# A four-layer graph network on one core: two more left products in seven blocks, block sums on another engine, and a different priority among ready work

## The chip, the cores and the metric

The kernel runs on one core of a Trainium2 chip. A core has five engines that work side by side, each on its own queue of instructions: TensorE (in the profile PE, with its weight loads as PEld), VectorE (DVE), ScalarE (ACT), GpSimd (POOL) and SyncE (SP), which here only issues DMAs. The metric is the device time of one execution in microseconds (us), the median of three runs.

## The reference

Input `x` is 64 graphs of 256 nodes with 128 features, in fp32, and `adj` a symmetric 256 x 256 matrix of zeros and ones. Four layers follow each other, each of the form `x = layernorm(x + layer(x, adj))`. The two that the change touches are:

```python
# layer 2: a gated unit, five steps; in_matrix = out_matrix = adj
m_in = jnp.einsum('nm,bmd->bnd', in_matrix, h)
m_out = jnp.einsum('nm,bmd->bnd', out_matrix, h)
av = jnp.concatenate([m_in, m_out], axis=-1)
u3 = h @ u3_w.T + u3_b
z = jax.nn.sigmoid(av @ w3_w.T + w3_b + u3)
r = jax.nn.sigmoid(av @ w4_w.T + w4_b + u3)
hv = jnp.tanh(av @ w5_w.T + w5_b + (r * h @ u5_w.T + u5_b))
h = (1.0 - z) * h + z * hv
# layer 3: powers one to three of adj, for two adjacencies that are both adj
nxt = jnp.einsum('ij,bjc->bic', adj, carry)        # three times
y_1 = jnp.einsum('bnik,iok->bno', x_all, weight_1) # x_all: x and the six products
```

Layers 0 and 1 are attention layers over the same adjacency. All arithmetic is fp32.

## The kernel before

**Tiling.** Two graphs make one unit: `UB = 2`, so there are `NU = 32` units. A unit's state is a 128 x 512 tile, features in the partitions and 2 x 256 nodes in the columns, or node-major, with the four blocks of 128 nodes (two graphs, two halves each) side by side. Ten units are in work at once, each in a lane with its own buffers (`LANES = 10`); matmul results lie in eight PSUM banks that all lanes share.

**The order.** Nothing is issued in the order in which the code is written. `add` (L85) records a task with its engine, an estimated duration, the cells that it reads and writes and, for a cell in PSUM, that it takes a bank (`takes`) or uses one (`banks`). `Plan.run` (L115) then plays the tasks through: at each moment every free engine takes, among its tasks whose inputs are due and for which a bank is free, the one with the smallest key. The key is `first` (L1017): the unit's number times `PERIOD` plus the task's due time within the unit; units of the last ten use a denser numbering. `tc.manual_schedule()` issues the result, so the order on each engine is fixed before the run and an instruction whose input is late holds up everything behind it on its engine. The plan's estimate for the time between the end of an instruction and its being seen by another engine (`LATENCY`) is 400 or 500 ns for the compute engines and 4000 for a DMA.

**A left product.** `left` (L812) multiplies a unit by the adjacency directly: for each graph two products of 256 columns, four in a unit. `left_fast` (L820) computes the same from seven products of 128 columns: the 2 x 2 block product with four block sums of the state (`four`, in the buffer `s`; VectorE, L826, L828 and L829), block sums of the matrix prepared once by `fast_blocks` (L466; `adjf` for plain node order and `adjTf` for permuted node order), one copy of the first product by ScalarE to `p1` (L845), and four merging sums by VectorE into `m` (L860, L863, L865, L866). The seven products are those at L833 and use two banks, `x` and `y`. `FAST` (L22) says where this form is used: steps 1 to 4 of layer 2 and (5) the first left product of layer 3. Step 0 of layer 2 uses `left` (L816) with one bank and a ScalarE copy at L886.

`far(u, step)` tells whether a unit's state goes from feature-major to node-major by DMA (through HBM) rather than by TensorE transposes. Units 0 and 1 go by DMA from step 2 on and unit 31 only up to step 0; `left_fast` is used only where `far` holds for the step before.

**A step of layer 2** (L868 to L958): the left product `m`; four 512-column products for the gates (`product`, L890, weights `gT`), the first of which, `gT[3]` with the old state, needs no `m` and follows the second matmul of the left product in the recorded dependencies; one more with `u5T`; three tanh on ScalarE (L901, L909, L918) and four `scalar_tensor_tensor` on VectorE (L904, L916, L920, L922), each over 128 x 512.

**Layer 3** (L970): the left product `aT`; then eight 256-column products with `w3` (L991), which holds the matrix for the part that needs no further adjacency and, beside it, the one for the part that is multiplied by the squared adjacency; ScalarE copies the second part to `s` (L995); four 256-column products with the squared adjacency `a2T` (L998) accumulate onto the first part in PSUM; `layernorm` reads the sum from PSUM. Units 30 and 31 use `layernorm_last`.

`layernorm` (L575): statistics on VectorE (L582), then for most units three small operations and a power on GpSimd (L584, L587, L593, L595), then ScalarE writes the normalised `x` (L606).

Of the kernel before, what the change touches and what calls it, by code (L numbers as in the profile page):

```python
# [13 lines left out]
P = 128  # L14
NEG = -1.0e30
EPS = 1e-5
STEPS = 5
# [1 line left out]
LEAD = 10  # L19
BANKS = 8  # L20
BL = 32
FAST = (1, 2, 3, 4, 5)  # L22
NORM = (0, 1, 2, 3)
SCALES = True
SMALL = ("ve", "cu", "d", "elu", "shift")
# [12 lines left out]
DIRECT_ROWS = 3  # L38
XDIRECT = 10
START = 35e3  # L40
R2 = 1
R3 = 1.5

# [157 lines left out]
def kernel(  # L201
# [42 lines left out]
    def sb(name, shape):  # L244
        return const.tile(shape, F32, tag=name, name=name)

    def cell(name, shape):
        return Cell(sb(name, shape))
# [4 lines left out]
    def bank():  # L253
        return Cell(bank=True)

    def mm_ns(cols, n=1):
        return n * (cols * 1.667 + 5)
# [115 lines left out]
            add(DVE, 200 + 100 * n, lambda: nc.vector.tensor_scalar_mul(t.ap, views(), scale), (ps,), (t,))  # L373
        return t

    adjT = cell("adjT", [P, NC, N])
    ps_adj = bank()
    for mc in range(NC):
        for ic in range(NC):
# [73 lines left out]
    add(POOL, 300, lambda: nc.gpsimd.tensor_scalar_mul(bias2.ap[:, 0:2], bias2.ap[:, 0:2], 0.5), (bias2,), (bias2,))  # L453


    adjTp, adj_p = cell("adjTp", [P, NC, N]), cell("adj_p", [P, NC * NC, BL, P // BL])
    add(ACT, 600, lambda: nc.scalar.copy(
        adj_p.ap, adj_t.ap.rearrange("p i (m q j) -> p (i m) j q", m=NC, j=BL)), (adj_t,), (adj_p,))
    ps_adjp = bank()
# [3 lines left out]
                ps_adjp.ap[:, mc * N + ic * P : mc * N + (ic + 1) * P],  # L463
                adj_p.ap[:, ic * NC + mc].rearrange("p j q -> p (j q)"), ident.ap), (adj_p, ident), (ps_adjp,))
    add(ACT, 500, lambda: nc.scalar.copy(adjTp.ap.rearrange("p c n -> p (c n)"), ps_adjp.ap), (ps_adjp,), (adjTp,))
    def fast_blocks(name, mat):  # L466


        f = cell(name, [P, 2 * NC, N])

        def block(k):
            return f.ap.rearrange("p k (c n) -> p (k c) n", c=NC)[:, k]

        add(ACT, 500, lambda: nc.scalar.copy(f.ap[:, 0:NC], mat.ap), (mat,), (f,))
        for out, (i, op, j) in {4: (1, ALU.subtract, 0), 6: (3, ALU.add, 1), 5: (6, ALU.subtract, 0)}.items():
            add(POOL, 480, lambda out=out, i=i, op=op, j=j: nc.gpsimd.tensor_tensor(block(out), block(i), block(j), op=op),
                (f,), (f,))

        add(POOL, 350, lambda: nc.gpsimd.tensor_scalar_mul(block(5), block(5), -1.0), (f,), (f,))
        add(POOL, 480, lambda: nc.gpsimd.tensor_add(block(7), block(5), block(2)), (f,), (f,))  # L480
        return f

    adjTf = fast_blocks("adjTf", adjTp)
    adjf = fast_blocks("adjf", adjT) if 0 in FAST or STEPS in FAST else None


    plan.rank = R3
    w3 = cell("w3", [D, 2, 2, D])
    add(POOL, 480, lambda: nc.gpsimd.tensor_add(w3.ap[:, 0, 0, :], wk.ap[:, :, 0], ident.ap), (wk, ident), (w3,))
    for k in range(1, 4):  # L490
        add(POOL, 480, lambda k=k: nc.gpsimd.tensor_add(
            w3.ap[:, k % 2, k // 2, :], wk.ap[:, :, k], wk.ap[:, :, k + 3]), (wk,), (w3,))

    a2T = cell("a2T", [P, NC, N])
    ps_a2 = bank()
    for mc in range(NC):
        for kc in range(NC):
# [2 lines left out]
                start=(kc == 0), stop=(kc == NC - 1)), (adj_t, adjT), (ps_a2,))  # L500
    add(DVE, 600, lambda: nc.vector.tensor_copy(a2T.ap.rearrange("p c n -> p (c n)"), ps_a2.ap), (ps_a2,), (a2T,))

    plan.rank = None


# [2 lines left out]
    def gd(ap):  # L508
        return ap.rearrange("p (g d) -> p g d", g=G)
# [307 lines left out]
                ps.ap[:, b * N : (b + 1) * N], lhs(b, mc), mat.ap[:, mc, :],  # L817
                start=(mc == 0), stop=(mc == NC - 1)), (src, mat), (ps,))

    def left_fast(src, blk, mat, s, p1, m):  # L820


        four = gd(s.ap)
        ss = object()

        add(DVE, 360, lambda: nc.vector.tensor_sub(  # L826
            four[:, 0:2], blk(slice(2, 3)).to_broadcast([P, 2, D]), blk(slice(0, 4, 3))), (src,), (s,), group=ss)
        add(DVE, 220, lambda: nc.vector.tensor_sub(four[:, 2:3], four[:, 1:2], blk(slice(0, 1))), (src, s), (s,), group=ss)  # L828
        add(DVE, 220, lambda: nc.vector.tensor_add(four[:, 3:4], four[:, 2:3], blk(slice(1, 2))), (src, s), (s,), group=ss)  # L829
        x, y = bank(), bank()  # L830

        def one(ps, at, lhs, k, c, cells, after=()):
            add(PE, mm_ns(P) + 4, lambda: nc.tensor.matmul(  # L833
                ps.ap[:, at * P : (at + 1) * P], lhs(), mat.ap[:, k, c * P : (c + 1) * P], start=True, stop=True,
                skip_group_check=True), (*cells, mat), (ps,), after, group=four)

        def a(g):
            return lambda: blk(slice(g, g + 1))[:, 0]

        def sm(k):  # L840
            return lambda: four[:, k]


        one(x, 0, a(0), 0, 0, (src,))
        add(ACT, 280, lambda: nc.scalar.copy(p1.ap[:, 0:P], x.ap[:, 0:P]), (x,), (p1,))  # L845
        one(x, 1, a(1), 1, 0, (src,))
        one(y, 3, a(3), 3, 1, (src,), s.writers[-1:])
        one(y, 1, sm(0), 3, 0, (s,))
        one(y, 0, sm(1), 2, 0, (s,))
        one(x, 2, sm(2), 2, 1, (s,))  # L850
        one(y, 2, sm(3), 1, 1, (s,))
        mv = gd(m.ap)

        ms = object()

        def pv(ps):
            return gd(ps.ap)


        add(DVE, 400, lambda: nc.vector.tensor_tensor(  # L860
            mv[:, 0:4:3], pv(x)[:, 1:3], p1.ap[:, 0:P].rearrange("p (o n) -> p o n", o=1).to_broadcast([P, 2, P]), op=ALU.add),
            (x, p1), (m,))
        add(DVE, 400, lambda: nc.vector.tensor_tensor(  # L863
            mv[:, 1:3], pv(y)[:, 0:2], mv[:, 3:4].to_broadcast([P, 2, P]), op=ALU.add), (y, m), (m,))
        add(DVE, 240, lambda: nc.vector.tensor_add(mv[:, 3:4], pv(y)[:, 0:1], mv[:, 2:3]), (y, m), (m,))  # L865
        add(DVE, 400, lambda: nc.vector.tensor_add(mv[:, 1:3], pv(y)[:, 2:4], mv[:, 1:3]), (y, m), (m,))  # L866

    def layer2(u, L):  # L868
        h, ht = turned(u, L, -1), X[u]
        for step in range(STEPS):  # L870
# [1 line left out]
            fast = step in FAST and far(u, step - 1)  # L872
            ps_m = None if fast else bank()
            if fast and not step:
                left_fast(ht, lambda g: ht.ap.rearrange("p b c d -> p (b c) d")[:, g], adjf, L["r"], L["z"], m)
            elif fast:
                left_fast(ht, lambda g: gd(ht.ap)[:, g], adjTf, L["r"], L["z"], m)
            for b in range(0 if fast else UB):
                if ht is X[u]:
                    left(ps_m, ht, b)  # L880
# [8 lines left out]
            def product(ps, w, c, rhs, start, stop, after=()):  # L889
                add(PE, mm_ns(T), lambda: nc.tensor.matmul(ps.ap, w(), rhs.ap, start=start, stop=stop,  # L890
                                                           skip_group_check=True), (c, rhs), (ps,), after)


            lefts = [t for t in plan.tasks[at:] if t.eng == PE]
            product(ps_g, lambda: gT.ap[:, 3], gT, h, True, False, lefts[1:2])
            product(ps_g, lambda: gT.ap[:, 1], gT, m, False, True)
            r, z, v = L["r"], L["z"], L["v"]

# [71 lines left out]
    def layer3(u, L):  # L970
        xT = turned(u, L, STEPS)
        aT, s = L["m"], L["z"]
        if STEPS in FAST and far(u, STEPS):
            left_fast(X[u], lambda g: X[u].ap.rearrange("p b c d -> p (b c) d")[:, g], adjf, L["r"], L["z"], aT)
            tail = [t for t in plan.tasks[-4:-3]]
        else:
            ps_a = bank()
            for b in range(UB):
                left(ps_a, X[u], b)
            add(ACT, 500, lambda: nc.scalar.copy(aT.ap, ps_a.ap), (ps_a,), (aT,))  # L980
            tail = list(ps_a.writers)

        ps = [bank() for _ in range(NC)]

        def view(c):
            return ps[c].ap.rearrange("p (k b d) -> p k b d", k=2, b=UB)

        for k, src in enumerate((xT, aT)):
            for c in range(NC):
                for b in range(UB):  # L990
                    add(PE, mm_ns(N), lambda k=k, src=src, c=c, b=b: nc.tensor.matmul(  # L991
                        view(c)[:, :, b, :], bn(src.ap)[:, b, c * P : (c + 1) * P], w3.ap[:, k],
                        start=(k == 0 and b == 0), stop=(k == 1), skip_group_check=True), (src, w3), (ps[c],), tail)
        for c in range(NC):
            add(ACT, 300, lambda c=c: nc.scalar.copy(s.ap[:, c * N : (c + 1) * N], ps[c].ap[:, N : 2 * N]), (ps[c],), (s,), group=ps)  # L995
        for c in range(NC):
            for mc in range(NC):
                add(PE, mm_ns(N), lambda c=c, mc=mc: nc.tensor.matmul(  # L998
                    ps[c].ap[:, 0:N], a2T.ap[:, mc, c * P : (c + 1) * P], s.ap[:, mc * N : (mc + 1) * N],
                    start=False, stop=(mc == NC - 1), skip_group_check=True), (a2T, s), (ps[c],))  # L1000
        pairs = [(ps[c], lambda c=c: view(c)[:, 0]) for c in range(NC)]
        if u >= NU - 2:
            layernorm_last(u, pairs)
            return
        layernorm(u, L, pairs, swap=True)
        add("sp", 450, lambda: nc.sync.dma_start(out_u[u], X[u].ap), (X[u],), ())
# [10 lines left out]
    def first(t):  # L1017
        if t.rank is not None:
            return t.rank * PERIOD
        if t.unit < 0:  # L1020
            return t.due - 1e6
        return (t.unit if t.unit < NU - LANES else NU - 1 - LATE - (NU - 1 - t.unit) * TAIL) * PERIOD + t.due

    with tc.manual_schedule():
        for t in plan.run(spawn, range(NU), first):
# [31 lines left out]
```

The softmax here doesn't subtract the row's maximum and nothing guards it: scores larger than these inputs give would overflow.

## Time and profile before

| What | Value |
|---|---|
| Median of three runs (lowest, highest) | 1395.11 us (1395.05, 1396.01) |
| Span of the profiled execution | 1394.1 us |
| ScalarE, the three tanh of layer 2 (L901, L909, L918), 160 each | 687 to 689 ns each |
| VectorE, `scalar_tensor_tensor` of a step (L904 to L922) | 683 to 687 ns each |
| VectorE, block sums: 128x256 (L826), 128x128 (L828, L829) | 411 and 399; 281 to 284 ns |
| VectorE, merging sums L860, L863, L866; L865 | 417, 418, 413; 281 ns |
| GpSimd, 128x128 block sums of the matrices (L476) | 467 and 491 ns |
| GpSimd, the layernorm power (L587), 126 times | 1127 ns |
| ScalarE copies L845, L886, L995 | 267, 585, 370 ns |

The span runs from the first to the last instruction of the profiled execution; the run's time has about one us around it. In the rows of the profile a name like `ps<-adjTf,e` says what is written and what is read, buffer numbers left out; since several names share one buffer, a row can show `e` where the code says `r` or `z`, and `p` where it says `v`. A matmul in fp32 appears as two records, a transpose as one. The mean duration in a group's row runs from a matmul's start to its modelled end, so that following matmuls overlap; their rate shows in how far apart they start. "Idle before" is time that the engine stood idle just before an instruction, with what ended it.

### The profile page before, as it was taken

What the parts mean: (1) busy time and instruction counts of PE and PEld (TensorE: products, weight loads), DVE (VectorE), ACT (ScalarE), POOL (GpSimd) and SP (SyncE); (2) the same over time, 40 slices, a digit from 0 to 9 for tenths busy, and PEclk for the clock granted to TensorE, in tenths of its full rate; (3) what the DMA queues carried; (4) which work ended last, traced back from release to release, by engine and by line L of the source; (5) the groups of instructions that cost most, each with busy time, mean ns of one, the idle gap of its engine ahead of it and who ended that gap; (6) DMA issues with size and microseconds to landing.
All of it is one profiled execution on the core that took longest, in us unless ns stands there. A gap on an engine that the chain in (4) does not pass through costs nothing.

```text
span 1394.1 us, 21842 instructions
## 1 busy us (share of the span) xinstructions
PE 1385.5 (99%) x6537; PEld 963.8 (69%) x6537; DVE 1191.1 (85%) x2849; ACT 911.2 (65%) x2094; POOL 257.9 (18%) x488
## 2 busy tenths in 40 slices
PE   9999999999999999999999999999999999999998
PEld 8776576776666766676676667676666666667776
DVE  6788898999988888888898899889888888999763
ACT  6887636556765767666676778787755555565454
POOL 3111020112112112122121122132111110112212
PEclk9999999999999999999999999999999999999999
DMA  4134554455455454554455555554463543544521
GB/s 126 32 62 99 114 120 86 117 108 131 109 114 112 98 130 95 122 127 102 108 108 111 128 110 110 118 114 103 108 129 94 119 105 86 115 114 106 129 52 47
DMA packets 530068, 147.03 MB, mean 105 GB/s; under 512 B 456480, under 2 KB 495136, under 8 KB 529952
## 3 DMA queue, kind: packets, MB, share of 16 engines
q1 hardware_dynamic: 529152, 145.13, 46.6%
q8 instruction: 52, 0.85, 0.3%
q14 instruction: 64, 0.52, 0.2%
q10 hardware_dynamic: 800, 0.52, 0.1%
HBM read 81.10 MB, written 64.46 MB: 104 GB/s over the span
## 4 chain that ended last, share of the span: by engine, by line
PE 98%; ACT 1%; DVE 1%; DMA 0%; issue 0%; SPq 0%; POOL 0%; POOLq 0%; DVEq 0%; ACTq 0%
PE ps L890 49%; PE ps L833 17%; PE ps L991 8%; PE ps L816 5%; PE ps L738 4%; PE ps L998 4%; PE ps L775 4%; PE ps L787 2%; PE ps L733 2%; PE ps L662 2%; ACT p L711 0%; DMA u<-rowu 0%; PE ps L348 0%; PE ps L955 0%; PE ps L528 0%; PE ps L571 0%
## 5 line engine op out<-in xcount | busy, mean ns | idle before, releaser
L890 PE MATMUL ps<-m,gT 128*128 128x512 f32 x960 | 464.1, 593 | 0.0
L890 PEld LDWEIGHTS ps<-m,gT 128*128 128x128 f32 x960 | 170.8, 190 | 124.9 <-issue 107.8
L909 ACT ACTIVATE e<-ps,bias 128x512 f32<-128x512 f32 x160 | 109.7, 687 | 159.0 <-PE ps L890 156.5
L901 ACT ACTIVATE e<-ps,bias 128x512 f32<-128x512 f32 x160 | 109.9, 687 | 98.9 <-PE ps L890 97.0
L833 PEld LDWEIGHTS ps<-adjTf,ht 128*128 128x128 f32 x726 | 117.6, 191 | 74.3 <-issue 60.1
L584 POOL TENSOR_SCALAR ve<-st 128x4 f32<-128x4 f32 x110 | 36.3, 330 | 690.5 <-DVE st L582 662.3
L890 PE MATMUL ps<-e,u5T 128*128 128x512 f32 x320 | 162.4, 592 | 0.0
L587 POOL TENSOR_TENSOR rstd<-ve,nhalf 128x4 f32<-128x4 f32 x126 | 142.0, 1127 | 66.5 <-DVE ve L584 59.5
L833 PEld LDWEIGHTS ps<-adjTf,e 128*128 128x128 f32 x968 | 127.4, 192 | 19.2 <-issue 17.7
L833 PE MATMUL ps<-adjTf,e 128*128 128x128 f32 x968 | 139.6, 275 | 0.0
L918 ACT ACTIVATE p<-ps,bias 128x512 f32<-128x512 f32 x160 | 110.2, 689 | 40.5 <-PE ps L890 38.4
L833 PE MATMUL ps<-adjTf,ht 128*128 128x128 f32 x726 | 123.7, 275 | 0.3 <-DVE m L860 0.3
L920 DVE SCALAR_TENSOR_TENSOR p<-e,p 128x512 f32<-128x512 f32 x160 | 109.4, 685 | 16.5 <-ACT p L918 16.0
L890 PEld LDWEIGHTS ps<-e,u5T 128*128 128x128 f32 x320 | 59.3, 190 | 61.4 <-issue 51.6
L890 PE MATMUL ps<-xT,gT 128*128 128x512 f32 x192 | 97.5, 594 | 0.4 <-ACT xT L530 0.4
L860 DVE TENSOR_TENSOR m<-ps,e 128x256 f32<-128x256 f32 x152 | 63.0, 417 | 25.1 <-PE ps L833 21.2
L764 ACT ACTIVATE e<-m,esd 128x256 f32<-128x256 f32 x116 | 82.2, 766 | 0.0
L904 DVE SCALAR_TENSOR_TENSOR e<-e,xT 128x512 f32<-128x512 f32 x96 | 65.7, 684 | 15.5 <-ACT e L901 13.5
L863 DVE TENSOR_TENSOR m<-ps,m 128x256 f32<-128x256 f32 x152 | 63.3, 418 | 16.0 <-PE ps L833 14.1
L541 DVE STREAM_TRANSPOSE p<-x 128x512 f32<-128x512 f32 x61 | 67.3, 1104 | 11.1 <-ACT x L606 11.0
L738 PEld LDWEIGHTS ps<-ht,p 128*128 128x128 f32 x512 | 65.9, 190 | 12.9 <-issue 12.0
L738 PE MATMUL ps<-ht,p 128*128 128x130 f32 x512 | 68.5, 274 | 0.0
(191 smaller groups left out, 2784.0 us busy)
## 6 DMA issues: line engine op xcount, KB each, us to landing
hb<-p SPq DMA_DIRECT2D x182, 256.0 KB, 2.3
ht<-hb SPq DMA_DIRECT2D x484, 64.0 KB, 2.6
xT<-hb SPq DMA_DIRECT2D x244, 64.0 KB, 2.5
m<-row SPq DMA_DIRECT2D x58, 256.0 KB, 3.8
hb<-p SPq DMA_DIRECT2D x124, 64.0 KB, 1.8
ht<-hb SPq DMA_DIRECT2D x31, 256.0 KB, 3.0
out_dram<-x SPq DMA_DIRECT2D x30, 256.0 KB, 2.4
m<-in_x_dram SPq DMA_DIRECT2D x88, 64.0 KB, 2.3
```

The lines of the kernel that those rows point to most:

```text
L541: add(DVE, 1050, lambda: nc.vector.transpose(v.ap.rearrange("p (a g i) -> p g a i", g=G, i=BL), X[u].ap.rearrange("p b c (j a) -> p (b c) ...
L587: add(POOL, 1050, lambda: nc.gpsimd.tensor_tensor(rstd.ap, ve.ap, nhalf.ap, op=ALU.pow), (ve, nhalf), (rstd,))
L738: add(PE, mm_ns(D + 2), lambda b=b, ic=ic, kc=kc, yv=yv: nc.tensor.matmul(yv()[:, ic, :], p.ap[:, b * NC + kc, ic * P : (ic + 1) * P], h.a ...
L764: add(ACT, 600, lambda g=g, b=b: nc.scalar.activation(e.ap[:, g, :].rearrange("p (c n) -> p c n", c=NC), ev()[:, b], AF.Prelu, bias=esd.ap ...
L816: add(PE, mm_ns(N), lambda b=b, mc=mc: nc.tensor.matmul(ps.ap[:, b * N : (b + 1) * N], lhs(b, mc), mat.ap[:, mc, :], start=(mc == 0), stop ...
L833: add(PE, mm_ns(P) + 4, lambda: nc.tensor.matmul(ps.ap[:, at * P : (at + 1) * P], lhs(), mat.ap[:, k, c * P : (c + 1) * P], start=True, st ...
L890: add(PE, mm_ns(T), lambda: nc.tensor.matmul(ps.ap, w(), rhs.ap, start=start, stop=stop, skip_group_check=True), (c, rhs), (ps,), after)
L901: add(ACT, 600, lambda ps_g=ps_g, up=up: nc.scalar.activation(r.ap, ps_g.ap, AF.Tanh, bias=bias2.ap[:, 1:2], scale=0.5 / up), (ps_g, bias2 ...
L909: add(ACT, 600, lambda ps_g=ps_g, up=up: nc.scalar.activation(z.ap, ps_g.ap, AF.Tanh, bias=bias2.ap[:, 0:1], scale=0.5 / up), (ps_g, bias2 ...
L918: add(ACT, 600, lambda ps_v=ps_v, up=up: nc.scalar.activation(v.ap, ps_v.ap, AF.Tanh, bias=bias2.ap[:, 2:3], scale=1 / up), (ps_v, bias2), ...
L920: add(DVE, 600, lambda: nc.vector.scalar_tensor_tensor(v.ap, z.ap, 1.0, v.ap, op0=ALU.add, op1=ALU.mult), (v, z), (v,))
L991: add(PE, mm_ns(N), lambda k=k, src=src, c=c, b=b: nc.tensor.matmul(view(c)[:, :, b, :], bn(src.ap)[:, b, c * P : (c + 1) * P], w3.ap[:, k ...
```

## The change

It has four parts. First, step 0 of layer 2 joins `FAST`, so that it uses `left_fast` with `adjf`. Second, a new branch of layer 3 for all but the last three units (`PLAIN = 3`) computes the product with the squared adjacency from seven 128-column products as well; its weights are block sums `a2f`, it adds block sums of `s` on VectorE (`-1` is not in `BY_POOL`), merges into the buffer `ht` in SBUF, and `layernorm` then reads from there. The last three units keep the old form in `layer3_end`, with the two halves of `w3` in the other order. Third, the block sums of the state are GpSimd's in all places named by `BY_POOL`. Fourth, the key of a task on TensorE, ScalarE or VectorE that uses an open bank without taking a new one becomes smaller by 10 us (`HASTE`). Two smaller parts: the block sums of a matrix now share one buffer with the matrix, so that two copies go; and the product with `gT[3]` depends, in the fast form, on the third merging sum in place of the second left matmul.

```diff
-FAST = (1, 2, 3, 4, 5)
+FAST = (0, 1, 2, 3, 4, 5)
+BY_POOL = (0, 1, 2, 3, 4, 5)
+HASTE = {"pe": 10e3, "act": 10e3, "dve": 10e3}
+PLAIN = 3
...
+    def blocks(name):
+        whole = Cell(sb(name, [P, 2 * NC, N]))
+        return whole, Cell(whole.ap[:, 0:NC])
+    adjf, adjT = blocks("adjT")
...
-        add(ACT, 500, lambda: nc.scalar.copy(f.ap[:, 0:NC], mat.ap), (mat,), (f,))
...
-    adjTf = fast_blocks("adjTf", adjTp)
-    adjf = fast_blocks("adjf", adjT) if 0 in FAST or STEPS in FAST else None
+    fast_blocks(adjTf, adjTp)
+    fast_blocks(adjf, adjT)
...
+    fast_blocks(a2f, a2T)
...
+    def block_sums(src, blk, s, by_pool):
+        four = gd(s.ap)
+        ss = object()
+        by, eng = (POOL, nc.gpsimd) if by_pool else (DVE, nc.vector)
+        wide, narrow = (830, 480) if by_pool else (360, 220)
-        add(DVE, 360, lambda: nc.vector.tensor_sub(
+        add(by, wide, lambda: eng.tensor_sub(
             four[:, 0:2], blk(slice(2, 3)).to_broadcast([P, 2, D]), blk(slice(0, 4, 3))), (src,), (s,), group=ss)
-        add(DVE, 220, lambda: nc.vector.tensor_sub(four[:, 2:3], four[:, 1:2], blk(slice(0, 1))), (src, s), (s,), group=ss)
-        add(DVE, 220, lambda: nc.vector.tensor_add(four[:, 3:4], four[:, 2:3], blk(slice(1, 2))), (src, s), (s,), group=ss)
+        add(by, narrow, lambda: eng.tensor_sub(four[:, 2:3], four[:, 1:2], blk(slice(0, 1))), (src, s), (s,), group=ss)
+        add(by, narrow, lambda: eng.tensor_add(four[:, 3:4], four[:, 2:3], blk(slice(1, 2))), (src, s), (s,), group=ss)
...
-            product(ps_g, lambda: gT.ap[:, 3], gT, h, True, False, lefts[1:2])
+            merge = plan.tasks[at:][-4:]
+            product(ps_g, lambda: gT.ap[:, 3], gT, h, True, False, merge[2:3] if fast else lefts[1:2])
...
+        if u >= NU - PLAIN:
+            layer3_end(u, L, xT, aT, s, tail)
+            return
+        x, y = bank(), bank()
+        home = {(0, 0): (x, slice(0, 2)), (1, 1): (x, slice(2, 4)), (0, 1): (y, slice(0, 3, 2)), (1, 0): (y, slice(1, 4, 2))}
+        for k, src in enumerate((xT, aT)):
+            for (b, c), (ps, at) in home.items():
+                add(PE, mm_ns(N), lambda k=k, src=src, c=c, b=b, ps=ps, at=at: nc.tensor.matmul(
+                    gd(ps.ap)[:, at], bn(src.ap)[:, b, c * P : (c + 1) * P], w3.ap[:, k],
+                    start=(k == 0 and b == 0), stop=(k == 1), skip_group_check=True), (src, w3), (ps,), tail)
+        four, sv = gd(L["xT1"].ap), gd(s.ap)
+        copies = object()
+        add(ACT, 370, lambda: nc.scalar.copy(sv[:, 0:4:3], gd(x.ap)[:, 0:3:2]), (x,), (s,), group=copies)
+        add(ACT, 370, lambda: nc.scalar.copy(sv[:, 1:3], gd(y.ap)[:, 0:2]), (y,), (s,), group=copies)
+        block_sums(s, lambda g: sv[:, g], L["xT1"], -1 in BY_POOL)
+        t, p1, out = L["xT1"], L["v"], L["ht"]
+        def one(ps, at, lhs, c, k, start, after=()):
+            return add(PE, mm_ns(P) + 4, lambda: nc.tensor.matmul(
+                ps.ap[:, at * P : (at + 1) * P], a2f.ap[:, k // NC, k % NC * P : (k % NC + 1) * P], lhs(), start=start,
+                stop=True, skip_group_check=True), (c, a2f), (ps,), after, group=four)
...
+        done = [one(x, 1, d(1), s, 2, False)]
+        one(x, 0, d(0), s, 0, True, done)
+        add(ACT, 280, lambda: nc.scalar.copy(p1.ap[:, 0:P], x.ap[:, 0:P]), (x,), (p1,))
+        done = [one(y, 3, d(3), s, 7, False), one(y, 2, sm(3), t, 3, False)]
+        one(y, 1, sm(0), t, 6, True, done)
+        one(y, 0, sm(1), t, 4, True, done)
+        one(x, 2, sm(2), t, 5, True, done)
+        merged(x, y, p1, out)
+        mv = gd(out.ap)
+        add(DVE, 240, lambda: nc.vector.tensor_add(mv[:, 3:4], gd(x.ap)[:, 3:4], mv[:, 3:4]), (x, out), (out,))
+        layernorm(u, L, y_pairs(out))
+        add("sp", 450, lambda: nc.sync.dma_start(out_u[u], X[u].ap), (X[u],), ())
...
-        return (t.unit if t.unit < NU - LANES else NU - 1 - LATE - (NU - 1 - t.unit) * TAIL) * PERIOD + t.due
+        soon = HASTE.get(t.eng, 0) if t.banks and not t.takes else 0
+        return (t.unit if t.unit < NU - LANES else NU - 1 - LATE - (NU - 1 - t.unit) * TAIL) * PERIOD + t.due - soon
```

`merged` is the four merging sums of `left_fast`, taken out into a function of its own.

## The prediction

> **What bounds the kernel now.** I read four views, in this order.
>
> First the page's summary: which engine is full.
>
> ```profile
> span 1394.1 us, 21842 instructions
> PE 1385.5 (99%) x6537; PEld 963.8 (69%) x6537; DVE 1191.1 (85%) x2849; ACT 911.2 (65%) x2094; POOL 257.9 (18%) x488
> ...
> DVE  6788898999988888888898899889888888999763
> ...
> PEclk9999999999999999999999999999999999999999
> ```
>
> TensorE is busy throughout at full clock (0.999 granted), and VectorE is second, above 90% in twelve slices of 40. GpSimd has most of its time free.
>
> A busy TensorE need not be a fast one, so second, what it waited for (the waits of PE: total, times, longest, in us):
>
> ```profile
> PE ps L348 <- POOL ident masks.py:199: 1.3, 1, 1.3
> PE ps L890 <- ACT xT L530: 0.4, 1, 0.4
> PE ps L662 <- ACT ht L665: 0.3, 1, 0.3
> PE ps L833 <- DVE m L860: 0.3, 1, 0.3
> PE ps L571 <- DVE cu L669: 0.2, 1, 0.2
> ```
>
> That is 2.5 us in the whole run. Taking the starts of successive matmul records and the usual distance for each width (112 ns for 128 columns, 216 for 256, 429 for 512), the distances alone make 1382.3 us of the 1386.3 us between first and last start. Four us are lost, nearly all before 80 us. So this is a matmul-issue-bound kernel: the time is a head of 1.3 us, the matmuls, and 6.5 us at the end from the last matmul's start to the last store.
>
> Third, what one matmul really costs. The group rows mislead here (mean ns of one is its latency, and busy per record counts overlaps):
>
> ```profile
> L833 PE MATMUL ps<-adjTf,e 128*128 128x128 f32 x968 | 139.6, 275 | 0.0
> L816 PE MATMUL ps<-adjT,x 128*128 128x256 f32 x264 | 67.0, 379 | 0.0
> ```
>
> By busy time a 128-column record costs 144 ns and a 256-column one 254, so that seven narrow products (two records each) would cost 2.02 us and four wide ones 2.03 us: no gain. The timeline has the truth; what counts is when the next group starts:
>
> ```profile
> 709.08 0.83 PE L833 MATMUL ps<-adjTf,e 128*128 128x128 f32 x6
> 709.75 0.83 PE L833 MATMUL ps<-adjf,e 128*128 128x128 f32 x6
> ...
> 1368.85 1.89 PE L998 MATMUL ps<-e,a2T 128*128 128x256 f32 x8
> 1370.58 1.03 PE L991 MATMUL ps<-w,xT 128*128 128x256 f32 x4
> ```
>
> Six narrow records take 0.67 us (112 ns each), eight wide ones 1.73 us (216 each).
>
> Fourth, the durations that price what moves to GpSimd, and a crowded stretch (busy us of PE, PEld, DVE, ACT, POOL with instruction counts; then clock, DMA share, GB/s):
>
> ```profile
> L476 POOL TENSOR_TENSOR adjf<-adjf 128x128 f32<-128x128 f32 x3 | 1.4, 491 | 6.9 <-ACT adjf L474 6.9
> L584 POOL TENSOR_SCALAR ve<-st 128x4 f32<-128x4 f32 x110 | 36.3, 330 | 690.5 <-DVE st L582 662.3
> ...
> 240.00:310.00 70.00, 70.00 (x343) 49.30 (x342) 67.65 (x168) 43.15 (x101) 10.96 (x17) 1.00 0.51 114
> ```
>
> VectorE is 97% busy from 240 to 310 us and TensorE still never waits.
>
> **What the Trainium skill says.** "Trainium Kernel Development and Optimization", Performance Expectations, warns that matmul busy time is a bad metric because matmuls are pipelined; the 144 ns against 112 ns above agree. "SBUF — State Buffer", Who interferes with whom, says that a VectorE instruction with two SBUF inputs (or in a two-port mode) and a GpSimd instruction that reads SBUF exclude each other for a whole instruction, and that the first to issue wins. This trace agrees on one side: L584's smallest duration is 194 ns, its mean 330, its largest 1637. On the other side VectorE's scalar_tensor_tensor rows (L904 to L922) keep 684 to 687 ns; but today's GpSimd operands have 4 columns. "GPSIMD Engine Reference", Performance versus the Vector engine, gives about 2.6 cycles an element for tensor_tensor.
>
> **The change, part by part.**
>
> TensorE. At step 0 of layer 2, L816's four 256-column products (eight records, 8 x 216 = 1.73 us) become seven of 128 columns (14 x 112 = 1.57 us): 0.16 us less. This holds for 30 units: 0 and 1 keep the old form at step 0 by `FIRST_FAR`. In layer 3, L998's four 256-column products become seven, in 29 units (all but the last three). The instruction order of the changed program has these counts: L816's products fall from 160 to 40, L998's from 128 to 12, the seven-block ones rise from 1064 to 1274 plus 203. L991 keeps 256 products of 256 columns. Sum: 59 x 0.163 = **9.6 us less** (0.160 with the rounded medians gives 9.4).
>
> VectorE. Removed: block sums L826, L828, L829, 49.6 + 12.4 + 34.1 + 8.7 + 34.4 + 8.8 = 148.0 us. Added: the four merging sums (0.417 + 0.418 + 0.281 + 0.413 = 1.53 us) in 59 places, 90.2 us; layer 3's own block sums, 29 x 0.98 = 28.3; one more 128-column sum, 29 x 0.28 = 8.1. Net -21 us: 1170.
>
> ScalarE. Step 0 trades an L886 copy (585 ns) for an L845 one (267): 30 x -0.32 = -9.5 us; layer 3 gains 29 x 0.27 = 7.7; two set-up copies at L474 go (1.2). Nothing in sum, on an engine with a third of its time free.
>
> GpSimd. 182 block sums come in (121 in the steps, 30 at step 0, 31 in layer 3): one 128x256 and two 128x128 operations each. Narrow: 0.45 to 0.49 (L476). Wide is not shown: from below 0.45, from above two narrow ones, 0.98; with the skill's 2.6 cycles at 1.2 GHz for 128 more elements I estimate 0.75. That is 1.7 us for one, 310 us in all; with the 0.06 to 0.14 us that the small rows lose on average to waiting, 2.0 us. POOL goes from 258 to about 600 us of 1385, 43%. One sum thus comes about 1.0 us later than VectorE's 0.98 us. Who waits: the matmuls that read it; and, queued behind it on GpSimd, the layernorm chain L584, L587, L593, L595, then ScalarE's L606. Cover: joining each L829 to the first matmul that reads it (152 pairs), the matmul starts at least 0.31 us later, 1.02 at the 5th percentile, 2.1 at the 25th, 3.8 at the median. Were nothing reordered, 1 us of delay would expose about 5% of 182, some 0.3 us each: 3 us. The order is planned anew with 1.79 us and 0.5 us of signal latency for it, so I take 0; bounds 0 and 3.
>
> The product of `gT[3]` (0.86 us) no longer follows the second left matmul but the third merging sum. It is 129 us of filler, tied closer to its unit's own chain. Behind it TensorE's whole queue waits. Bounds: 0, and 150 x 0.7 (the sums L865 and L866 uncovered) = 105; I take 0, because TensorE waited for VectorE's `m` 0.3 us in the entire run and ten units supply other work. Its bank opens later, which helps. No DMA is added or dropped; SP's queue only changes its order.
>
> The preference for open banks can win at most the 4 us lost at the start, or lose some: I take 0, bounds -3 and +3. Set-up gains five GpSimd operations for the squared adjacency (2.5 us), before layer 3 needs them. The end keeps the old form, so its tail stays.
>
> Sum: span 1394.1 - 9.6 = 1384.5. The run's median lies 1.0 us above the profiled span: **1385.5 us**.
>
> **Rivals.**
> 1. Part is given back: late sums and tied products expose 3 to 7 us. For it: VectorE above 90% in twelve slices; GpSimd's 1637 ns outlier. Against: the slack above. 1388.5 to 1392.3, say 1390.
> 2. No difference: the seven blocks save nothing, as busy time says (2.02 against 2.03 us): 1395. The timeline speaks against it; only losses of about 9 us by rival 1's route would end there.
> 3. Slower: the shared port makes VectorE the bound. If half of GpSimd's new 310 us blocks VectorE, its load rises by 155/1385 = 0.11; in the twelve slices near 0.95 (418 us), 0.95 - 0.015 + 0.11 = 1.045, so 19 us are missing there: 1404. It outweighs the saving once blocking takes about 0.09 of VectorE's time there. Against: a GpSimd operation is caught about a fifth of the time; random meetings cost some 900 port-taking VectorE instructions x 0.22 x 0.3 us = 60 us, a load of 0.04, which still fits.
> 4. Better: the new order also removes the start's losses: 1382.
>
> **How the numbers follow.** Forecast (1383.5 to 1388) 0.66; rival 1, 0.09; rival 2, 0.07; rival 3, 0.13; rival 4, 0.05. The range 1382.5 to 1392 holds the forecast, rival 1 and little more: about 0.8. A measurement of this kernel tells 0.2% (2.8 us) from no change. Faster: 0.66 + 0.09 + 0.05 = 0.80; same 0.07; slower 0.13.
>
> **What would show it.** Right: matmul records rise by 354 to 6891, waits of PE stay under 5 us, POOL near 600, DVE near 1170. The port: scalar_tensor_tensor means well above 687, DVE above 1230. Wrong: PE waits naming POOL block sums or `m`, or gaps inside the seven-block groups; 128-column records spaced over 112 ns where squared-adjacency blocks are the weights.

## The result, and the profile after

| | Before | After |
|---|---|---|
| Median of four runs (lowest, highest) | 1395.56 us (1395.05, 1396.54) | 1391.27 us (1391.07, 1392.14) |
| Span of the profiled execution | 1394.1 us | 1390.3 us |
| Distances between matmuls alone | 1382.3 us | 1373.0 us |
| Lost between matmuls | 4.0 us | 10.0 us |

The ratio is 0.9968, with a 95% interval of 0.9954 to 0.9982: a gain of 4.3 us where 9.6 were forecast. The time lies near the upper end of the stated range (1382.5 to 1392), in the part that belonged to rival 1. The profiled execution of the changed kernel is the slowest of the four, 0.9 us above their median. The two last rows are worked out as in the prediction, from the starts of successive matmul records. About 1.1 of the 6.0 us by which the loss grew are no wait: TensorE's first matmuls start at twice their later distance, until 5.0 us in the profile before and until 7.2 us in this one (the last section has the figures).

The page's summary of the changed kernel (busy time, share, instructions; then VectorE's load in 40 slices):

```profile
span 1390.3 us, 23222 instructions
PE 1379.5 (99%) x6891; PEld 967.8 (70%) x6891; DVE 1217.7 (88%) x2745; ACT 909.1 (65%) x2121; POOL 630.5 (45%) x1039
...
DVE  6887999999888989989898999899889798988955
```

TensorE has the 6891 records that were counted, and POOL about the 600 us. VectorE, which should have come down to 1170 us, went up to 1217.7. The waits of PE (total, times, longest):

```profile
PE ps L351 <- POOL ident masks.py:199: 1.3, 1, 1.3
PE ps L792 <- DVE m L872: 0.7, 1, 0.7
...
PE ps L902 <- DVE m L878: 0.5, 1, 0.5
...
PE ps L902 <- DVE m L872: 0.5, 1, 0.5
PE ps L844 <- ACT e L856: 0.4, 1, 0.4
...
```

Before, apart from the first line, no wait was above 0.4 us and one named VectorE's merging sums; now three do. None names GpSimd's block sums; nine weight loads waited for one, 2.7 us in all on PEld, and the matmuls after them started on time. The groups by form show what VectorE has become (mean ns of one after the busy time), first a line of the kernel before, then the changed kernel:

```profile
L920 DVE SCALAR_TENSOR_TENSOR p<-e,p 128x512 f32<-128x512 f32 x160 | 109.4, 685 | 16.5 <-ACT p L918 16.0
```

```profile
L933 DVE SCALAR_TENSOR_TENSOR p<-e,p 128x512 f32<-128x512 f32 x160 | 117.2, 733 | 33.1 <-ACT p L931 32.1
L833 POOL TENSOR_TENSOR e<-ht 128x256 f32<-128x256 f32 x121 | 99.4, 821 | 89.0 <-DMA ht<-hb 67.9 <-PE ps L902 10.0 <-PE ps L844 5.0
L835 POOL TENSOR_TENSOR e<-e,ht 128x128 f32<-128x128 f32 x121 | 79.4, 657 | 5.9
```

The 128x512 `scalar_tensor_tensor` (L920 before, L933 now) takes 733 ns in place of 685, and GpSimd's sums take 821 and 657 ns where their shortest ones take 719 and 447. Both engines' instructions are stretched. The stretching goes with the overlap: of the 672 `scalar_tensor_tensor` of 128x512 in this profile, the 231 that overlap a block sum in time take 831 ns on average, and the other 441 take 681 ns, none of them more than 716. One such place in the timeline (start, duration):

```profile
167.05 1.18 POOL L833 TENSOR_TENSOR e<-ht 128x256 f32<-128x256 f32 x1
...
167.56 1.21 DVE L933 SCALAR_TENSOR_TENSOR p<-e,p 128x512 f32<-128x512 f32 x1
...
168.31 0.78 POOL L835 TENSOR_TENSOR e<-e,ht 128x128 f32<-128x128 f32 x1
...
168.70 0.94 DVE L917 SCALAR_TENSOR_TENSOR e<-e,xT 128x512 f32<-128x512 f32 x1
...
169.17 0.79 POOL L836 TENSOR_TENSOR e<-e,ht 128x128 f32<-128x128 f32 x1
...
169.56 0.94 DVE L935 SCALAR_TENSOR_TENSOR p<-p 128x512 f32<-128x512 f32 x1
...
172.49 0.41 DVE L872 TENSOR_TENSOR m<-ps,e 128x256 f32<-128x256 f32 x1
...
172.95 0.71 PE L792 MATMUL ps<-wx,xT 128*128 128x129 f32 x4 [0.72 <-DVE m L872]
```

Read it downwards: a block sum of GpSimd is under way when VectorE's L933 starts, which then lasts 1.21 us in place of 0.69. The next two pairs do the same, 0.94 us each. VectorE works without a pause through this stretch (busy 10.0 of the 10.0 us from 166 to 176), so the 1.0 us are not caught up: three microseconds later a product of another unit waits 0.72 us for a merging sum that frees its bank.

### The profile page after: what moved, and what is told of

It is laid out like the page before. It is cut to its first block, busy times and chain, and to the rows that moved or that the text cites. A ratio compares the mean times of both kernels' runs of the same rounds, so it can differ in the third digit from the quotient of the medians.

```text
span 1390.3 us, 23222 instructions
## 1 busy us (share of the span) xinstructions
PE 1379.5 (99%) x6891; PEld 967.8 (70%) x6891; DVE 1217.7 (88%) x2745; ACT 909.1 (65%) x2121; POOL 630.5 (45%) x1039
## 4 chain that ended last, share of the span: by engine, by line
PE 94%; DVE 3%; ACT 1%; POOL 0%; issue 0%; DMA 0%; POOLq 0%; SPq 0%; DVEq 0%; ACTq 0%
PE ps L902 48%; PE ps L844 20%; PE ps L1004 7%; PE ps L780 4%; PE ps L743 4%; PE ps L1015 3%; PE ps L792 2%; PE ps L738 2%; PE ps L667 2%; PE ps L821 1%; PE ps L1048 1%; PE ps L1055 0%; DVE st L587 0%; PE ps L351 0%; PE ps L968 0%
## 5 line engine op out<-in xcount | busy, mean ns | idle before, releaser
L844 PE MATMUL ps<-adjTp,e 128*128 128x128 f32 x968 | 148.2, 275 | 0.4 <-ACT e L856 0.4
L933 DVE SCALAR_TENSOR_TENSOR p<-e,p 128x512 f32<-128x512 f32 x160 | 117.2, 733 | 33.1 <-ACT p L931 32.1
L844 PEld LDWEIGHTS ps<-adjTp,e 128*128 128x128 f32 x968 | 131.0, 192 | 19.0 <-issue 14.5
L833 POOL TENSOR_TENSOR e<-ht 128x256 f32<-128x256 f32 x121 | 99.4, 821 | 89.0 <-DMA ht<-hb 67.9
L844 PEld LDWEIGHTS ps<-adjTp,ht 128*128 128x128 f32 x726 | 108.7, 191 | 40.8 <-issue 36.7
L844 PE MATMUL ps<-adjTp,ht 128*128 128x128 f32 x726 | 120.8, 275 | 0.0
L611 ACT ACTIVATE x<-ht,ve,rstd 128x128 f32<-128x128 f32 x212 | 90.9, 487 | 13.9 <-POOL ve L600 13.6
L833 POOL TENSOR_TENSOR e<-x 128x256 f32<-128x256 f32 x61 | 48.2, 790 | 96.2 <-ACT x L611 83.9
L875 DVE TENSOR_TENSOR m<-ps,m 128x256 f32<-128x256 f32 x182 | 74.8, 413 | 13.4 <-PE ps L844 11.1
L872 DVE TENSOR_TENSOR m<-ps,e 128x256 f32<-128x256 f32 x182 | 74.4, 413 | 11.2 <-PE ps L844 6.9
L835 POOL TENSOR_TENSOR e<-e,ht 128x128 f32<-128x128 f32 x121 | 79.4, 657 | 5.9
```

The costliest lines, as they stand in the source:

```text
L611: add(ACT, 400, lambda j=j, b=b, ch=ch, view=view, at=at, shift=shift, col=col: nc.scalar.activation(X[u].ap[:, b, ch, :], view()[:, j, :] ...
L833: add(by, wide, lambda: eng.tensor_sub(four[:, 0:2], blk(slice(2, 3)).to_broadcast([P, 2, D]), blk(slice(0, 4, 3))), (src,), (s,), group=ss)
L835: add(by, narrow, lambda: eng.tensor_sub(four[:, 2:3], four[:, 1:2], blk(slice(0, 1))), (src, s), (s,), group=ss)
L844: add(PE, mm_ns(P) + 4, lambda: nc.tensor.matmul(ps.ap[:, at * P : (at + 1) * P], lhs(), mat.ap[:, k, c * P : (c + 1) * P], start=True, st ...
L933: add(DVE, 600, lambda: nc.vector.scalar_tensor_tensor(v.ap, z.ap, 1.0, v.ap, op0=ALU.add, op1=ALU.mult), (v, z), (v,))
```

## The experiments

Each kernel ran beside the kernel before on the same chip; the medians of the kernel before lay between 1395.65 and 1395.93 us. "Lost" is the time between matmuls beyond their usual distances, in the profiled execution.

### The same order, with GpSimd's reads taken away

`thin_sums`:

```diff
+        w = 1 if by_pool else D
...
-            four[:, 0:2], blk(slice(2, 3)).to_broadcast([P, 2, D]), blk(slice(0, 4, 3))), (src,), (s,), group=ss)
+            four[:, 0:2, 0:w], blk(slice(2, 3))[:, :, 0:w].to_broadcast([P, 2, w]), blk(slice(0, 4, 3))[:, :, 0:w]), (src,), (s,), group=ss)
...
```

The two narrow sums are cut to one column likewise. The planned durations stay, so the order stays: in the traces TensorE, VectorE, ScalarE and the DMA queue run through the same operations in the same sequence as in the changed kernel, in both kernels of this section.

> The changed kernel with every instruction in the same order, but GpSimd's block sums one column wide (2, 1 and 1 columns in place of 256, 128 and 128); the matmuls read what the buffer held before, so the left products are not computed. Measured so far: changed kernel 1391.3 us, kernel before 1395.6; 9.3 us of matmul distances are gone, but the time lost between matmuls rose from 4.0 to 10.0 us. Theory PORT (GpSimd's reads block VectorE, whose 128x512 scalar_tensor_tensor rose from 685 to 733 ns, and VectorE then comes late where it is crowded): back to 686 ns, DVE busy near 1170 us, about 1386.5 us. Theory LATE (the sums themselves come too late): also about 1386.5 us. Theory ORDER (the new priority and the new plan, not GpSimd, open the gaps): 1390.5 to 1391.5 us.

`memset_sums`:

```diff
+        if by_pool:
+            def wait_and_set():
+                eng.tensor_copy(four[:, 0:1, 0:1], blk(slice(2, 3))[:, :, 0:1])
+                eng.memset(s.ap, 0.5)
+            add(by, wide, wait_and_set, (src,), (s,), group=ss)
+            add(by, narrow, lambda: eng.memset(s.ap, 0.5), (src, s), (s,), group=ss)
+            add(by, narrow, lambda: eng.memset(s.ap, 0.5), (src, s), (s,), group=ss)
+            return four
```

> The changed kernel with the same order, but each GpSimd block sum replaced by write-only work of about the same length: a one-column copy that reads the state and a memset of the buffer's 512 columns, then two more such memsets; the sums are not computed. GpSimd keeps some 1.5 to 1.7 us for each sum but reads almost nothing. PORT: VectorE's scalar_tensor_tensor back to 686 to 690 ns, DVE near 1170 us, time about 1386.5 us. LATE: as slow as the changed kernel, 1391 us, since the matmuls wait as long for GpSimd. ORDER: 1391 us.

Measured: `thin_sums` 1388.23 us (1387.81 to 1388.79; ratio to before 0.9945, 0.9930 to 0.9960), `memset_sums` 1388.64 us (1387.97 to 1389.04; ratio 0.9947, 0.9932 to 0.9962). Neither range meets that of the changed kernel, though the intervals of the ratios overlap at their edges (0.9954 to 0.9960 or 0.9962). Groups by form of `memset_sums`:

```profile
L836 POOL MEMSET e<- 128x512 f32 x182 | 95.5, 525 | 10.8
...
L942 DVE SCALAR_TENSOR_TENSOR p<-e,p 128x512 f32<-128x512 f32 x160 | 109.5, 685 | 39.5 <-ACT p L940 38.8
```

GpSimd is busy for 588.8 us, against 630.5 in the changed kernel, and three such memsets take 1.58 us; yet VectorE is back at 685 ns and at 1180.7 us (1179.5 in `thin_sums`). Stretches 160 to 200 and 240 to 320 us (busy us of PE, PEld, DVE, ACT, POOL with counts; clock; DMA), first the changed kernel, then `thin_sums`, then `memset_sums`:

```profile
160.00:200.00 40.00, 39.28 (x201) 27.80 (x200) 36.99 (x85) 20.93 (x43) 20.30 (x29) 1.00 0.49 111
240.00:320.00 80.00, 78.43 (x380) 53.67 (x379) 74.22 (x167) 51.37 (x122) 35.01 (x55) 1.00 0.48 108
```

```profile
160.00:200.00 40.00, 40.00 (x200) 27.87 (x200) 34.24 (x88) 21.39 (x44) 10.61 (x30) 1.00 0.51 111
240.00:320.00 80.00, 79.41 (x389) 54.77 (x388) 72.43 (x174) 51.24 (x121) 18.31 (x54) 1.00 0.51 114
```

```profile
160.00:200.00 40.00, 40.00 (x204) 28.12 (x204) 34.27 (x88) 21.50 (x45) 18.67 (x37) 1.00 0.50 110
240.00:320.00 80.00, 79.41 (x389) 54.58 (x388) 72.46 (x172) 51.89 (x122) 32.50 (x66) 1.00 0.51 114
```

TensorE's gap of 0.7 us in the first stretch is gone in both, and of the 1.6 us in the second, 1.0 are. What makes VectorE late is that GpSimd reads, not how long GpSimd takes: PORT stands, and its price in this order is 3.0 us. The two profiles give the same figure: 10.0 us lost in the changed kernel and 5.9 in `thin_sums`, and 1.1 of these 4.1 us is the start at half rate, which in `thin_sums` ends at 5.1 us. Three waits for merging sums (L872 twice, L878), which cost 2.5 us with the slow matmul after each, are gone from the profile of `thin_sums`.

Little is left for LATE. The stand-in's 1.58 us is what an undisturbed block sum takes (0.72 + 0.45 + 0.45), and the further 0.5 us of the real one is stretching that goes with the same overlap (the narrow sums that meet a `scalar_tensor_tensor` of 128x512 take 716 ns on average, the others 479); the profile of `memset_sums` has one wait of 0.3 us for a stand-in, and its median is 0.4 us above that of `thin_sums`.

That VectorE keeps its 685 ns is what the Trainium skill's "SBUF — State Buffer", Who interferes with whom, says of an instruction that only writes: it does not contend with one that has two SBUF inputs. But both kernels stay 1.7 to 2.1 us above the 1386.5 that PORT alone would give. That rest is not the port's.

The waits of PE in `thin_sums`, then those in `order_only` (described below; no block sum on GpSimd, another plan):

```profile
PE ps L576 <- DVE cu L674: 0.7, 1, 0.7
PE ps L667 <- ACT xT L535: 0.6, 1, 0.6
PE ps L845 <- ACT e L857: 0.4, 1, 0.4
PE ps L792 <- ACT xT L783: 0.2, 1, 0.2
```

```profile
PE ps L576 <- DVE cu L674: 0.7, 1, 0.7
PE ps L667 <- ACT xT L535: 0.6, 1, 0.6
PE ps L844 <- DVE e L835: 0.4, 1, 0.4
PE ps L792 <- ACT xT L783: 0.2, 1, 0.2
```

Both lists leave out the 1.3 us at the start, which the kernel before has too. The first two lines lie in the attention layers, near 17 and 39 us, and are alike in both plans; in the kernel before, the wait for `cu` was 0.2 us, and its wait of 0.4 us for `xT` came at 46 us, at another product.

### Undoing the two rules of order

```diff
-HASTE = {"pe": 10e3, "act": 10e3, "dve": 10e3}
+HASTE = {}
```

> The changed kernel without the 10 us preference for open banks; everything is computed and the plan makes a new order. ORDER by this preference: about 1386 us, lost time between matmuls back to about 4 us. PORT or LATE: 1390 to 1394 us, the loss stays or grows, VectorE's scalar_tensor_tensor stays near 733 ns.

```diff
-            product(ps_g, lambda: gT.ap[:, 3], gT, h, True, False, merge[2:3] if fast else lefts[1:2])
+            product(ps_g, lambda: gT.ap[:, 3], gT, h, True, False, lefts[1:2])
```

> The changed kernel with the gT[3] product again after the second left matmul in place of the third merging sum; everything is computed. Theory TIED (that product was filler, and its new place exposes the merging sums): about 1387 us. PORT, LATE: 1390 to 1394 us; earlier banks may cost a little more.

Both expectations of a gain failed. `no_haste` 1406.03 us (1403.26 to 1406.88; ratio 1.0065, 1.0049 to 1.0082), `early_h` 1402.09 us (1401.66 to 1403.54; ratio 1.0046, 1.0031 to 1.0061). Lost: 24 and 20 us, of which 10 and 8 us lie after 1360 us. TensorE in `no_haste` there:

```profile
1378.57 1.06 PE L844 MATMUL ps<-adjT,e 128*128 128x128 f32 x8
1381.00 0.66 PE L968 MATMUL ps<-ident,p 128*128 128x128 f32 x4 [1.38 <-DVE p L935]
1383.23 3.75 PE L1048 MATMUL ps<-w,xT 128*128 128x256 f32 x8 [1.57 <-DMA xT<-hb]
```

With few units left, their chains stand open: eight records fill 0.9 us, then the next ones wait for a transpose's input and for a DMA. In the changed kernel the loss after 1360 us is 0.25 us. So nothing speaks for the preference or the later `gT[3]` product as the cost: each plan without one of them is worse, above all at the end. Since each edit also draws a new order over the whole run, their 14.8 and 10.8 us are not the price of one rule alone, and a small cost of TIED inside the changed kernel's own order is not excluded by this.

### Undoing the other parts, one at a time

```diff
-BY_POOL = (0, 1, 2, 3, 4, 5)
+BY_POOL = ()
```

> The changed kernel with all block sums on VectorE (new plan); everything is computed. VectorE would carry 1218 - 47 + 182 x 0.98 = 1350 us of work, no port conflict. If the port costs more than it relieves (PORT as a reason against the move): 1388 us or less. If the move to GpSimd is what makes the rest possible: VectorE is 97% full and TensorE waits for it, 1395 to 1420 us.

```diff
+DVE_REAL = 1.2
...
+        if eng == "dve":
+            ns *= DVE_REAL
         t = Task(eng, ns, fn, self.unit, wait, dma or eng == "sp")
```

> The changed kernel with the plan's durations of VectorE tasks times 1.2 (600 becomes 720 ns; the trace has 733 for the scalar_tensor_tensor, 702 for the transposes), so that the fixed order reckons with the port; everything is computed. If the port's 3 us come from an order that expects VectorE too early: 1388 us. If the port costs throughput that no order gives back, or if a new order only draws other gaps: 1391 us or more.

```diff
-FAST = (0, 1, 2, 3, 4, 5)
+FAST = (1, 2, 3, 4, 5)
```

> The changed kernel with step 0 of layer 2 as before (four products of 256 columns, no block sums on GpSimd there, 30 units); everything is computed. By the matmul count: 30 x 0.163 = 4.9 us more, less what the port gives back (30 of 182 sums, 0.5 us): 1395.7 us. If step 0's part is lost to waits anyway: 1391 us.

```diff
-PLAIN = 3
+PLAIN = 32
```

> The changed kernel with layer 3's squared-adjacency product as before in all units (four products of 256 columns); everything is computed. By the matmul count 29 x 0.163 = 4.7 us more; but VectorE loses 29 x 2.8 = 81 us of work, which takes the crowding away. If the remaining loss (2 us besides the port's 3) sits in VectorE's load: 1391 to 1392 us, a gain that equals the loss. If not: 1396 us.

| Kernel | Median (lowest, highest), us | Ratio to before (interval) | DVE busy, us | Lost, us |
|---|---|---|---|---|
| sums_on_dve | 1413.80 (1413.00, 1414.95) | 1.0128 (1.0112 to 1.0145) | 1290.8 | 31.6 |
| real_dve | 1435.00 (1434.16, 1435.90) | 1.0280 (1.0265 to 1.0295) | 1210.4 | 52.3 |
| old_step0 | 1396.31 (1395.70, 1397.15) | 1.0003 (0.9994 to 1.0011) | 1183.8 | 9.5 |
| old_layer3 | 1394.20 (1393.42, 1395.29) | 0.9989 (0.9982 to 0.9996) | 1153.0 | 6.8 |

`sums_on_dve`: the move to GpSimd costs 3 us at the port and still pays; the plan without it is 22.5 us slower than the changed kernel. VectorE came to 1290.8 us and not to the 1350 that adding durations had given. Busy time counts instructions that overlap once (in this kernel's timeline a VectorE instruction of 0.41 us starts at 298.82 and the next at 299.16), so a denser VectorE's busy time rises by less than that sum. The traces confirm it: the durations of VectorE's instructions add up to 1395.4 us in the changed kernel and to 1523.0 in this one, so that the part counted once grew from 178 to 232 us, nearly the whole of the 59 us that were missing. From 280 to 320 us of this kernel:

```profile
280.00:320.00 40.00, 35.67 (x160) 23.98 (x160) 36.82 (x101) 22.71 (x54) 5.04 (x8) 0.91 0.53 113
```

TensorE stands still for 4.3 us of 40, and the granted clock is 0.91 there.

`real_dve` failed plainly: an order planned with VectorE's times all 1.2 times as long lost five times as much as the changed kernel's. So nothing supports the thought that the plan's short estimates cause the loss; why the longer ones do this much harm stays open.

`old_step0` gives back 5.0 us, as the count of matmuls says (4.9, less what the port frees). `old_layer3` gives back 2.9 of 4.7: layer 3's seven blocks are worth less than their matmuls. The rest, 1.8 us, comes back as fewer waits, in a plan that spares VectorE 65 us; the profiles show 3.2 us less lost, of which 0.9 is the longer half-rate start in the changed kernel's profile.

### One part alone, and near orders

`pool_only`: `FAST = (1, 2, 3, 4, 5)`, `PLAIN = 32`, `HASTE = {}` and the `gT[3]` dependency as before, so that the block sums' engine differs from the kernel before. `order_only`: `BY_POOL = ()`, with the same `FAST` and `PLAIN`, so that the two rules of order remain. Both also keep the changed set-up (shared matrix buffers, block sums of the squared adjacency that nothing then reads, the swapped halves of `w3`), so neither is one part quite alone.

> Of the change only the move of the block sums to GpSimd (152 sums; step 0, layer 3, the preference and the gT[3] dependency as before); everything is computed. TensorE's work is that of the kernel before, 1395.9 us with 4 us lost, so there is nothing to win but those. PORT: VectorE's scalar_tensor_tensor near 725 ns, VectorE 1191 - 148 + 40 = 1080 us and no longer crowded, so the port costs little by itself: 1395 to 1398 us. If a blocked VectorE stalls TensorE wherever it stands: 1399 us or more.

> Of the change only the order: the preference for open banks, the gT[3] product after the third merging sum, and the matrices' shared buffers; all block sums on VectorE, step 0 and layer 3 as before; everything is computed. At most the 4 us lost between matmuls can be won: 1393 to 1396 us. If the new order is what costs (ORDER): above 1397 us.

```diff
-HASTE = {"pe": 10e3, "act": 10e3, "dve": 10e3}
+HASTE = {"pe": 8e3, "act": 8e3, "dve": 8e3}
```

> The changed kernel with a preference of 8 us in place of 10: a new plan with the same work, to see how far two near orders lie apart. If the order's gaps are a matter of luck: 1388 to 1400 us, different from 1391.3 by more than 2 us. If the preference acts smoothly: 1391 to 1393 us.

> The changed kernel with a preference of 12 us. Luck: as for 8 us, 1388 to 1400 us. Smooth: 1390.5 to 1391.5 us.

> The changed kernel with a preference of 16 us; everything is computed. 8, 10 and 12 us gave 1393.0, 1391.3 and 1390.0. If the preference acts in one direction: 1388 to 1390 us. If two near orders lie apart by luck: anything from 1388 to 1400 us.

Then `pool_only` and `haste_12` with the one-column sums of `thin_sums`, each in its own order:

> pool_only (1401.0 us) with the same order, but GpSimd's block sums one column wide, so that the left products of steps 1 to 4 and of layer 3 are not computed. If pool_only's 5 us over the kernel before are the port's: 1396 us. If they are the new order's: 1400 us or more.

> haste_12 (1390.0 us) with the same order, but GpSimd's block sums one column wide (left products not computed). If the port costs about 3 us whatever the order: 1387 us. If it cost that in the order of the changed kernel alone: 1389 to 1390 us.

| Kernel | Median (lowest, highest), us | Ratio to before (interval) | Lost, us |
|---|---|---|---|
| pool_only | 1400.99 (1400.06, 1401.73) | 1.0036 (1.0023 to 1.0049) | 8.2 |
| pool_only_thin | 1399.25 (1398.17, 1399.51) | 1.0023 (1.0014 to 1.0033) | 7.1 |
| order_only | 1397.39 (1396.70, 1398.49) | 1.0011 (1.0004 to 1.0018) | 6.1 |
| haste_8 | 1393.01 (1392.35, 1394.98) | 0.9979 (0.9971 to 0.9987) | 10.6 |
| haste_12 | 1389.95 (1389.77, 1390.61) | 0.9958 (0.9943 to 0.9973) | 7.7 |
| haste_12_thin | 1388.61 (1387.93, 1389.73) | 0.9950 (0.9935 to 0.9965) | 5.6 |
| haste_16 | 1390.37 (1389.48, 1391.34) | 0.9962 (0.9947 to 0.9977) | 8.0 |

Moving the sums makes the kernel 5.1 us slower, of which holding the order and thinning the sums gives back 1.7; `pool_only_thin` is still 3.6 us slower than the kernel before, which is left to its new order and the set-up. In `haste_12` the port costs 1.3 us. So the port's price is 3.0, 1.7 and 1.3 us in three orders: always a loss, and no fixed one. `order_only` shows that the two rules bring nothing without the other parts: it is 1.5 us slower than the kernel before, just above the 1397 us that were expected if the new order is what costs. Preferences of 8, 10, 12 and 16 us lie within 3.1 us of each other; 12 gave the lowest median of all kernels that compute everything, 1.3 us below the changed kernel. The ranges of the two do not meet, though the intervals of their ratios to before overlap. Whether the preference acts in one direction or near plans differ by luck is not decided: 16 us gave neither a further gain nor a wide swing.

## Why the prediction was half right

**TensorE's term was right.** 59 places at 0.163 us were to save 9.6 us; the distances between matmuls fell by 9.3. So rival 2, that the seven blocks save nothing, falls. The seven-block groups run at the assumed rate with the squared adjacency as weights too:

```profile
706.80 0.39 PE L1015 MATMUL ps<-p,a2T 128*128 128x128 f32 x2
707.02 1.06 PE L792 MATMUL ps<-wx,xT 128*128 128x129 f32 x8
```

Two records take 0.22 us.

**The step that failed: port contention and the new order were put at zero.** Rival 3's mechanism is at work: 60 us of blocking were estimated, and in the same order VectorE's busy time is 1217.7 us with GpSimd's reads and 1179.5 in `thin_sums` without most of them: 38 us. The estimate took 900 instructions, a chance of 0.22 and 0.3 us each; of the `scalar_tensor_tensor`, 231 of 672 (0.34) met a block sum and lost 0.15 us each. It was thus too large by a factor of 1.6, and that is not what failed. The error was the conclusion, that a load "which still fits" costs nothing, and the port then had no term in the sum. VectorE needs no load of 1 to hold up TensorE: the order is fixed, VectorE has stretches without a pause, and delays of 0.3 to 0.5 us there pass through the following instructions to a merging sum that some product waits for. The measured price is 3.0 us. The signs named beforehand came in part: `scalar_tensor_tensor` well above 687 ns and waits that name `m`, while VectorE's load stayed under 1230 us and TensorE's waits, at 4.9 us in all, under 5. The loss has the size of rival 1 (3 to 7 us) but, as far as the experiments show, not its causes, late sums and tied products; that the time fell into its range is in that sense luck.

**The second missing term is the order.** The prediction took 0 for the new plan, with bounds of -3 and +3, and the cost lies within them. In the changed kernel's own order, `thin_sums` stands at 1388.23 where 1395.6 - 9.3 = 1386.3 would have been: 1.9 us. This is what the port's term leaves, so the sum -9.3 + 3.0 + 1.9 must come out near the measured -4.3; two other figures support it. The profile of `thin_sums` has 5.9 us lost where the one before has 4.0, with starts at half rate of the same length: 1.4 us more in the first 40 us, 1.0 less in the next 40, 1.2 more between 240 and 320, 0.3 more after 1360. And `order_only` is 1.5 us slower than the kernel before, with the same two waits in the attention layers, for `cu` and for `xT`. Which part of the change draws these waits is not shown; the one for `cu`, 0.6 us, is also in `pool_only`, which has no preference for open banks, so it need not come from that rule.

**What was rightly put at zero.** Late sums: GpSimd's 2.0 us for a sum (measured 821 + 657 + 622 ns = 2.1 us; undisturbed, the wide one takes 0.72 us where 0.75 were estimated) cost little by their lateness, since the write-only stand-in of 1.58 us gave 1388.64 against 1388.23, and no wait of PE in the changed kernel names them. The tied `gT[3]` product, with a bound of 105 us, cost nothing that an experiment shows; undone, the kernel was slower. The cover used in the argument, a median of 3.8 us between a sum and its first reader, held for the sums and said nothing of the merging sums, the tanh inputs and the banks that late VectorE work sets free. That was the wrong slack to look at.

## What to carry to other kernels

When work moves to GpSimd beside a busy VectorE, price what VectorE's instructions with two SBUF inputs lose, then look for the stretches where VectorE has no pause: there the loss reached TensorE here, although the average load was 88%. With an order fixed in advance, test a suspected cost by thinning the operation while its planned duration stays, so that the order stays; edits that make a new plan moved this kernel by 1 to 44 us, and how much of that is the plan's cannot be told from such a run alone. Judge narrow against wide matmuls by the distance of their starts, never by busy time.

## What the runs showed of the hardware that was not expected

Blocking between VectorE and GpSimd works both ways in one run: 128x512 `scalar_tensor_tensor` instructions rose from about 680 to as much as 1251 ns, and 128x128 sums on GpSimd from 447 to as much as 2051 ns, while memsets of 512 columns on GpSimd took 525 ns and left VectorE at 685. GpSimd's shortest operations were stretched too: in `thin_sums` the one-column sums took 190 ns in the median and up to 1784, beside `scalar_tensor_tensor` instructions that kept 683 ns.

TensorE's first matmuls run at half their later rate: records of 256 columns start 427 ns apart where later ones start 216 apart. Where this ends differs from profile to profile: at 5.0 us in the profile before, at 7.2 us in the one after, and between 4.2 and 6.9 us in the others. Each further microsecond costs half a microsecond, so by these figures it makes 1.1 us between the two main profiles and 1.5 at most. The clock column of the profile reads 1.00 in these windows, so the slow start shows in the distances alone.
